# Pairwise products with batch statistics: the statistics computed with one shift per input, with half-sums on GpSimd

## The chip, the cores and the metric

The kernel runs on one core of one Trainium2 chip. The metric is device time in microseconds of one execution. A core has five engines that run side by side, each with its own instruction queue: TensorE (PE; its weight loads are shown as PEld), VectorE (DVE), ScalarE (ACT), GpSimd (POOL) and SyncE (SP), which here only issues transfers. Transfers run on 16 DMA engines. SBUF is the on-chip memory with 128 partitions; PSUM takes what TensorE makes.

## The reference

The inputs xi and xj are 1024 x 39 x 16 in float32. For each of the 741 pairs of a row r and a smaller column c, the outer product of xj[:, r] and xi[:, c] (16 x 16) is normalized over the batch and over both feature axes, scaled and shifted by gamma and beta of the pair, and multiplied by a 16 x 16 weight W:

```python
cross = xj[:, rows, :, None] * xi[:, cols, None, :]
mean = jnp.mean(cross, axis=(0, 2, 3), keepdims=True)
var = jnp.mean(jnp.square(cross - mean), axis=(0, 2, 3), keepdims=True)
normed = (cross - mean) * jax.lax.rsqrt(var + BN_EPS)
normed = normed * gamma[None, :, None, None] + beta[None, :, None, None]
out = normed[:, :, None, :, :] * W[None, None, :, :, :]
```

The output has 1024 x 741 x 256 values, 777 MB.

## The kernel before, in words

The batch lies as 128 partitions of NT = 8 rows each (index t), and is worked on T = 2 rows at a time. The kernel has two stages.

**Statistics.** The mean and variance of a product over the batch follow from small matrices of sums: per row t, the sum over the 16 features of each of the G = 38 used fields (`total`), and the sum of their squares. To keep the squares small, a shift per field is subtracted first; the shift is the field's mean over the rows t = 0. `sums` (L356) reduces the 16 features on VectorE. `deviation` (L366) subtracts the shift on GpSimd into a scratch tile; `square` (L375) squares that tile in place on ScalarE; `moments` (L381) sums the squares over the 16 features on VectorE; `means` (L388) makes the shifted means on VectorE. `gram` (L399) then accumulates three 38 x 77 matrices over the rows t on TensorE (`ps_g`). There are four pairs of rows for each of the two inputs, so eight deviations, squares and moments. From the three matrices a few 38 x 38 steps on ScalarE, GpSimd and VectorE (L478 to L508) make the mean and 1/std of every pair (`stq`), with one square root on ScalarE (L503).

**Spreading.** `spread` (L515) copies rows of that 38 x 38 table to all partitions with 76 matmuls in 12 groups, and `apply` (L531) combines a group with gamma and beta in `st_sb`. The first group (row 19) is needed first.

**Products.** A tile n holds T rows of the batch and the pairs of one row r: tile 0 to 3 are the row r = 19 (`mid`), later tiles other rows. `product` (L147) is one instruction of ScalarE or GpSimd: one row t and one feature i of xj times all r fields of xi. Tile 0 is special: its products are made from the raw xi while the statistics still run. These are 32 instructions of 128 x 304 elements, `raw0` on ScalarE (24 of them) and `raw0_pool` on GpSimd (8), handed out in portions by `emit` at places of the order that is written out by hand (L408 to L504). After `st_sb` is ready, `affine` (L241) scales and shifts tile 0 pair by pair on ScalarE, GpSimd and VectorE, and `weigh` (L254) multiplies by W on VectorE and stores in pieces. Since each raw product writes one feature of all 19 pairs, `affine` needs all 32. For later tiles `scale_xi` (L169) scales xi by the pair's factor on GpSimd, `products` (L183) multiplies on ScalarE and GpSimd, and `finish` (L276) adds the shift and multiplies by W, most of it on VectorE (L313), a share on GpSimd (L299, L302). `store` (L225) issues the output transfers on SP.

The order on every engine is that in which the program text issues instructions (`tc.manual_schedule()`); each engine works its queue in that order, so an instruction that waits holds up what stands behind it on its engine. Buffers are fixed: `y_sb` holds the output tiles in two halves, and the scratch of the statistics lies in the parts of it that the first tiles do not use yet. A transfer waits, before it is issued, for the transfer eight before it.

Input loads are issued on two queues: xj on SP, xi on ACT, between ScalarE's activations; gamma, beta and W also on ACT, after the fourth and fifth square (L449, L452).

Of the kernel before, what the change touches and what calls it, by code (L numbers as in the profile page):

```python
# [14 lines left out]
T = 2  # L15
# [12 lines left out]
LOADS = (1, 2, 3, 4, 6, 8)  # L28
# [15 lines left out]
def tile_pair_outer_batchnorm(  # L44
# [58 lines left out]
    place = {"dev": half * EE, "rest": (half + half // 2) * EE}  # L103
    stop = {"dev": (half + half // 2) * EE, "rest": 2 * half * EE}
# [18 lines left out]
    devs = [scratch("dev", P, T, G, E) for _ in range(7)]  # L123
# [5 lines left out]
    shift = scratch("rest", P, 2, G)  # L129
    shift_r = scratch("rest", G, 1)  # L130
    g1 = scratch("rest", G, 2 * G + 1)
    u_u, u_2 = (scratch("rest", G, 1) for _ in range(2))
    k, q1, q2, q3, uv, uv_2, v_half, mixed, low, mean, rstd, inv = (scratch("rest", G, G) for _ in range(12))
# [189 lines left out]
    with tc.manual_schedule():  # L323
        nc.gpsimd.memset(ones, 1.0)
        nc.sync.dma_start(xi_sb[:, 0, 0 : F // 2], xi_v[:, 0, 0 : F // 2])
        nc.scalar.dma_start(xi_sb[:, 0, F // 2 : F], xi_v[:, 0, F // 2 : F])
        nc.sync.dma_start(xj_sb[:, 0], xj_v[:, 0])
        def load(engine, to, source, t0, t1):
            engine.dma_start(to[:, t0:t1], source[:, t0:t1])

        for t0, t1 in zip(LOADS, LOADS[1:-2]):
            load(nc.sync, xj_sb, xj_v, t0, t1)
            load(nc.scalar, xi_sb, xi_v, t0, t1)


        nc.scalar.activation(shift_r, ones[0:G, 0:1], AF.Sqrt)
        load(nc.sync, xj_sb, xj_v, *LOADS[-3:-1])
# [12 lines left out]
        k_s = 1.0 / (P * E)  # L350
        sources = (xj_sb[:, :, 1:F], xi_sb[:, :, 0:G])

        def part(x):
            return slice(x * G, (x + 1) * G)

        def sums(t0, t1, xs=(1, 0)):  # L356
            for x in xs:
                nc.vector.tensor_reduce(  # L358
                    total[:, t0:t1, part(x)], sources[x][:, t0:t1], AX.X, ALU.add
                )  # L360

        steps = ((0, 1), (0, 0), (2, 1), (4, 1), (6, 1), (2, 0), (4, 0), (6, 0))

        def deviation(n):  # L366
            t0, x = steps[n]
            nc.gpsimd.tensor_tensor(  # L368
                devs[n % 7],
                sources[x][:, t0 : t0 + T],  # L370
                shift[:, x : x + 1, :].unsqueeze(3).to_broadcast([P, T, G, E]),
                ALU.subtract,
            )

        def square(n):  # L375

            _, x = steps[n]
            scale = 0.25 / NB**0.5 if x else 0.25
            nc.scalar.activation(devs[n % 7], devs[n % 7], AF.Square, scale=scale)  # L379

        def moments(n, t0, t1):  # L381
            first_t, x = steps[n]
            to = fb if x else fa
            nc.vector.tensor_reduce(  # L384
                to[:, t0:t1, G : 2 * G], devs[n % 7][:, t0 - first_t : t1 - first_t], AX.X, ALU.add
            )

        def means(t0, t1):  # L388
            for x, to in enumerate((fa, fb)):
                stt(  # L390
                    to[:, t0:t1, 0:G],
                    total[:, t0:t1, part(x)],
                    1.0 / (E * NB) if x else 1.0 / E,
                    ps_u[:, x : x + 1, :].to_broadcast([P, t1 - t0, G]),
                    ALU.mult,
                    ALU.subtract,
                )

        def gram(n, t0, t1):  # L399
            x = steps[n][1]  # L400
            for t in range(t0, t1):
                terms = ((0, fa[:, t, 0:G]), (2, ones[:, 0:G])) if x else ((1, fa[:, t, G : 2 * G]),)
                for acc, lhs in terms:
                    nc.tensor.matmul(  # L404
                        ps_g[acc][0:G, 0 : 2 * G + 1], lhs, fb[:, t], start=t == 0, stop=t == NT - 1
                    )

        raw0 = raw_products(0, nc.scalar, range(24))  # L408
        raw0_pool = raw_products(0, nc.gpsimd, range(24, 32))
        ps_shift = (ps_g[0][:, 0:G], ps_s[:, 0:G])  # L410
        for x in (1, 0):
            sums(0, 1, (x,))
            nc.tensor.matmul(ps_shift[x], ones, total[:, 0, part(x)], start=True, stop=True)
        nc.tensor.matmul(ps_c[0:G, 0:1], total[:, 0, 0:G], ones[:, 0:1], start=True, stop=True)

        ps_u = ps_s[:, 2 * G : 4 * G].rearrange("p (x f) -> p x f", x=2)
        nc.scalar.activation(shift[:, 1], ps_shift[1], AF.Copy, scale=k_s)
        nc.scalar.activation(ps_u[:, 1], shift[:, 1], AF.Copy, scale=1.0 / NB)
        load(nc.scalar, xi_sb, xi_v, *LOADS[-3:-1])
        load(nc.sync, xj_sb, xj_v, *LOADS[-2:])  # L420
        nc.scalar.activation(shift[:, 0], ps_shift[0], AF.Copy, scale=k_s)
        nc.scalar.copy(ps_u[:, 0], shift[:, 0])
        nc.scalar.activation(shift_r, ps_c[0:G, 0:1], AF.Copy, scale=k_s)

        def cell(n):
            return ps_c[0:G, 64 + n * G : 64 + (n + 1) * G]

        p_v_2, p_y, p_var, p_a, p_b = (cell(n) for n in range(5))
        u, v = shift_r, shift[0:G, 1, :]
        nc.scalar.activation(v_half, v, AF.Copy, scale=0.5)  # L430
        nc.scalar.activation(p_v_2, v, AF.Copy, scale=2.0)
        nc.scalar.activation(u_u, u, AF.Square)
        nc.scalar.activation(u_2, u, AF.Copy, scale=2.0)
        nc.scalar.activation(uv, v, AF.Copy, scale=u)
        nc.scalar.activation(uv_2, v, AF.Copy, scale=u_2)
        load(nc.scalar, xi_sb, xi_v, *LOADS[-2:])
        sums(1, 2)
        means(0, 2)
        sums(2, 3)
        sums(3, 4)  # L440
        means(2, 4)
        for n in range(7):
            deviation(n)
        emit(raw0, 2)
        for n in range(len(steps)):
            square(n)
            if n == 3:

                nc.scalar.dma_start(st_sb[:, 0], gamma.partition_broadcast(P))  # L449
                nc.scalar.dma_start(st_sb[:, 1], beta.partition_broadcast(P))  # L450
            elif n == 4:
                nc.scalar.dma_start(  # L452
                    w_sb[:, 0, :], w.rearrange("o i j -> (o i j)").partition_broadcast(P)
                )
            elif n < len(steps) - 1:
                emit(raw0, 2)

            t0 = steps[n][0]
            ends = (t0, t0 + 1, t0 + T) if n == len(steps) - 1 else (t0, t0 + T)
            for t0, t1 in zip(ends, ends[1:]):  # L460
                moments(n, t0, t1)
                gram(n, t0, t1)
            if n == 0:
                deviation(7)
            elif n == 1:
                sums(4, 6)
            elif n == 2:
                sums(6, 8)
                means(4, 8)
        emit(raw0_pool, 4)  # L470
# [6 lines left out]
        e_ab, e_a = g1[:, 0:G], g1[:, 2 * G : 2 * G + 1]  # L477
        nc.scalar.copy(g1, ps_g[0][0:G, 0 : 2 * G + 1])  # L478
        nc.scalar.activation(k, ps_g[2][0:G, 0:G], AF.Copy, scale=u)
        nc.scalar.activation(q1, v, AF.Copy, scale=e_a)  # L480
        nc.scalar.activation(q2, ps_g[2][0:G, G : 2 * G], AF.Copy, scale=u_u)
        nc.scalar.activation(q3, ps_g[0][0:G, G : 2 * G], AF.Copy, scale=u_2)
        emit(raw0, 3)
        nc.scalar.copy(w_dve, w_sb)
        emit(raw0, 4)
        nc.gpsimd.tensor_tensor(k, k, q1, ALU.add)
        nc.gpsimd.tensor_tensor(k, k, e_ab, ALU.add)
        nc.gpsimd.tensor_tensor(q2, q2, q3, ALU.add)
        nc.gpsimd.tensor_tensor(q3, uv_2, e_ab, ALU.mult)
        nc.gpsimd.tensor_tensor(q2, q2, q3, ALU.add)  # L490
        nc.gpsimd.tensor_tensor(q1, k, k, ALU.mult)
        nc.gpsimd.tensor_tensor(q2, q2, q1, ALU.subtract)
        nc.gpsimd.tensor_tensor(mean, k, uv, ALU.add)
        emit(raw0_pool, 4)

        stt(mixed, v_half, ps_g[1][0:G, 2 * G : 2 * G + 1], ps_g[1][0:G, 0:G], ALU.mult, ALU.add)
        nc.vector.tensor_mul(p_y, mixed, p_v_2)
        stt(low, ps_g[1][0:G, G : 2 * G], BN_EPS, q2, ALU.add, ALU.add)
        nc.vector.tensor_add(low, p_y, low)
        nc.vector.tensor_scalar_max(p_var, low, BN_EPS)  # L500

        nc.vector.reciprocal(inv, p_var)
        nc.scalar.activation(rstd, inv, AF.Sqrt)  # L503
        emit(raw0, 32)  # L504
        nc.vector.tensor_mul(p_a, p_var, rstd)
        stt(p_b, p_a, -0.5, rstd, ALU.mult, ALU.mult)
        stt(stq[:, 0], p_b, 1.5, rstd, ALU.add, ALU.mult)
        stt(stq[:, 1], mean, -1.0, stq[:, 0], ALU.mult, ALU.mult)  # L508

# [83 lines left out]
```

## Time and profile before

| | us |
|---|---|
| median of 4 runs | 1874.27 (1874.18 to 1874.43) |
| the profiled execution's own time | 1874.33 |
| its span, first to last instruction | 1872.6 |
| VectorE / ScalarE / GpSimd busy | 1723.0 / 1584.4 / 1550.9 |
| TensorE busy | 26.0 |
| read / written | 6.00 MB / 776.99 MB, 418 GB/s over the span |

The page gives busy time by engine, the span in 40 slices, the transfers, and groups of instructions by source line with mean duration and the idle time before them. The timeline lists instructions in order of time, neighbours of one line merged. "L153" is line 153 of the kernel; a line in a helper such as `product` stands for all its callers, which the operands tell apart: `y_sb<-xi_sb,xj_sb` on L153 is a raw product of tile 0, `y_sb<-xs,xj_sb` one of a later tile. `y_sb` as a destination of the first 30 us is mostly scratch.

### The profile page before, as it was taken

What the parts mean: (1) busy time and instruction counts of PE and PEld (TensorE: products, weight loads), DVE (VectorE), ACT (ScalarE), POOL (GpSimd) and SP (SyncE); (2) the same over time, 40 slices, a digit from 0 to 9 for tenths busy, and PEclk for the clock granted to TensorE, in tenths of its full rate; (3) what the DMA queues carried; (4) which work ended last, traced back from release to release, by engine and by line L of the source; (5) the groups of instructions that cost most, each with busy time, mean ns of one, the idle gap of its engine ahead of it and who ended that gap; (6) DMA issues with size and microseconds to landing.
All of it is one profiled execution on the core that took longest, in us unless ns stands there. A gap on an engine that the chain in (4) does not pass through costs nothing. (4 is left out here: it accounts for less than half of the span.)

```text
span 1872.6 us, 9236 instructions
## 1 busy us (share of the span) xinstructions
PE 26.0 (1%) x130; PEld 23.2 (1%) x130; DVE 1723.0 (92%) x2641; ACT 1584.4 (85%) x3152; POOL 1550.9 (83%) x1650
## 2 busy tenths in 40 slices
PE   5000000000000000000000000000000000000000
PEld 4000000000000000000000000000000000000000
DVE  8999888899999999999999999999999999999994
ACT  8999888898888877666798999999899998989892
POOL 9999877787777788999988888888888888888882
DMA  5999999999999999999999999999999999999998
GB/s 214 390 418 425 428 427 426 422 426 427 426 427 426 428 425 428 426 428 423 422 426 425 426 432 427 425 432 425 426 431 425 430 426 429 427 429 426 429 427 355
DMA packets 54711, 783.61 MB, mean 418 GB/s; under 512 B 4720, under 2 KB 6384, under 8 KB 17520
## 3 DMA queue, kind: packets, MB, share of 16 engines
q1 hardware_dynamic: 53344, 779.72, 98.2%
q10 hardware_dynamic: 1296, 3.29, 0.5%
q14 instruction: 70, 0.57, 0.1%
q8 instruction: 1, 0.02, 0.0%
HBM read 6.00 MB, written 776.99 MB: 418 GB/s over the span
## 5 line engine op out<-in xcount | busy, mean ns | idle before, releaser
L313 DVE SCALAR_TENSOR_TENSOR y_sb<-y_sb,st_sb,w_dve 128x512 f32<-128x512 f32 (+1 forms) x2511 | 1653.0, 738 | 114.4 <-issue 96.4
L153 ACT ACTIVATE y_sb<-xs,xj_sb 128x144 f32<-128x144 f32 (+23 forms) x2930 | 1453.3, 586 | 239.2 <-DMA out_dram<-y_sb 206.0
L302 POOL TENSOR_TENSOR y_sb<-y_sb,w_sb 128x2048 f32<-128x2048 f32 (+3 forms) x155 | 517.5, 3345 | 89.9 <-ACT y_sb L297 80.4
L155 POOL TENSOR_SCALAR y_sb<-xs,xj_sb 128x320 f32<-128x320 f32 (+19 forms) x1006 | 557.6, 578 | 9.1 <-DMA out_dram<-y_sb 9.0
L175 POOL TENSOR_TENSOR xs<-xi_sb,st_sb 128x640 f32<-128x640 f32 (+33 forms) x135 | 183.9, 1363 | 180.2 <-ACT y_sb L153 175.5
L299 POOL TENSOR_SCALAR y_sb<-y_sb,st_sb 128x512 f32<-128x512 f32 x291 | 196.8, 691 | 5.1 <-ACT y_sb L153 5.1
L297 ACT ACTIVATE y_sb<-y_sb,st_sb 128x512 f32<-128x512 f32 x160 | 100.2, 709 | 3.8 <-POOL y_sb L155 2.2
L208 POOL TENSOR_TENSOR y_sb<-xs,xj_sb 128x1280 f32<-128x1280 f32 (+2 forms) x24 | 66.6, 2798 | 0.0
L198 DVE TENSOR_TENSOR y_sb<-xs,ps 128x256 f32<-128x256 f32 (+3 forms) x32 | 24.8, 817 | 0.5
L522 PE MATMUL ps<-y_sb 38*128 38x38 f32 (+37 forms) x76 | 16.4, 397 | 3.1 <-DVE y_sb L508 3.1
L522 PEld LDWEIGHTS ps<-y_sb 38*128 38x128 f32 x76 | 16.3, 329 | 3.3 <-DVE y_sb L508 3.3
L379 ACT ACTIVATE y_sb<-y_sb 128x1216 f32<-128x1216 f32 x8 | 9.7, 1211 | 3.1 <-POOL y_sb L368 1.8
L153 ACT ACTIVATE y_sb<-xi_sb,xj_sb 128x304 f32<-128x304 f32 x24 | 11.4, 540 | 0.0
L384 DVE TENSOR_REDUCE y_sb<-y_sb 128x76 f32<-128x1216 f32 (+1 forms) x9 | 10.9, 1268 | 0.0
L259 DVE TENSOR_TENSOR y_sb<-y_sb,w_dve 128x2048 f32<-128x2048 f32 (+4 forms) x6 | 10.7, 1837 | 0.1
L368 POOL TENSOR_TENSOR y_sb<-xi_sb,y_sb 128x1216 f32<-128x1216 f32 x4 | 9.0, 2262 | 1.3 <-DMA xi_sb<-in_r_xi_dram 1.1
L358 DVE TENSOR_REDUCE y_sb<-xi_sb 128x38 f32<-128x608 f32 (+1 forms) x6 | 5.9, 990 | 3.9 <-DMA xi_sb<-in_r_xi_dram 3.9
L368 POOL TENSOR_TENSOR y_sb<-xj_sb,y_sb 128x1216 f32<-128x1216 f32 x4 | 9.0, 2265 | 0.0
L404 PE MATMUL ps<-y_sb 128*38 128x77 f32 x48 | 8.1, 337 | 13.4 <-DVE y_sb L384 13.2
L252 POOL TENSOR_SCALAR y_sb<-y_sb,st_sb 128x512 f32<-128x512 f32 x8 | 6.4, 812 | 2.0 <-ACT y_sb L153 2.0
L250 ACT ACTIVATE y_sb<-y_sb,st_sb 128x512 f32<-128x512 f32 x9 | 6.5, 799 | 0.2 <-ACT y_sb L153 0.2
L358 DVE TENSOR_REDUCE y_sb<-xj_sb 128x38 f32<-128x608 f32 (+1 forms) x6 | 5.9, 991 | 0.6 <-DMA xj_sb<-in_r_xj_dram 0.4
(60 smaller groups left out, 42.8 us busy)
## 6 DMA issues: line engine op xcount, KB each, us to landing
out_dram<-y_sb SPq DMA_DIRECT2D x16, 3072.0 KB, 21.7
out_dram<-y_sb SPq DMA_DIRECT2D x20, 2432.0 KB, 12.5
out_dram<-y_sb SPq DMA_DIRECT2D x10, 4608.0 KB, 15.1
out_dram<-y_sb SPq DMA_DIRECT2D x12, 3840.0 KB, 21.0
out_dram<-y_sb SPq DMA_DIRECT2D x16, 2816.0 KB, 22.3
out_dram<-y_sb SPq DMA_DIRECT2D x12, 3584.0 KB, 23.1
out_dram<-y_sb SPq DMA_DIRECT2D x12, 3328.0 KB, 24.3
out_dram<-y_sb SPq DMA_DIRECT2D x15, 2560.0 KB, 11.9
```

The costliest lines, as they stand in the source:

```text
L153: nc.scalar.activation(y, src, AF.Copy, scale=scale)
L155: engine.tensor_scalar(y, src, scale, 1.0, ALU.mult, ALU.mult)
L175: nc.gpsimd.tensor_tensor(xs, xi_sb[:, t0 : t0 + T, 0:r, :], s_sb[:, :, n0 : n0 + r, :].to_broadcast([P, T, r, E]), ALU.mult,)
L198: nc.vector.tensor_tensor(view(n)[:, t].rearrange("p n (i j) -> p n i j", j=E), xs[:, t].unsqueeze(2).to_broadcast([P, r, E, E]), xj_short ...
L208: nc.gpsimd.tensor_tensor(view(n)[:, t].rearrange("p n (i j) -> p n i j", j=E), xs[:, t].unsqueeze(2).to_broadcast([P, r, E, E]), xj_sb[:, ...
L297: nc.scalar.activation(y[:, :, c, :], y[:, :, c, :], AF.Identity, bias=t_c)
L299: nc.gpsimd.tensor_scalar(y[:, :, c, :], y[:, :, c, :], t_c, 1.0, ALU.add, ALU.mult)
L302: nc.gpsimd.tensor_tensor(y[:, :, c0:c1, :], y[:, :, c0:c1, :], w_sb.unsqueeze(1).to_broadcast([P, T, c1 - c0, EE]), ALU.mult,)
L313: stt(y[:, t : t + size, c, :], y[:, t : t + size, c, :], t_sb[:, n0 + c : n0 + c + 1], w_dve.to_broadcast([P, size, EE]), ALU.add, ALU.mult,)
L358: nc.vector.tensor_reduce(total[:, t0:t1, part(x)], sources[x][:, t0:t1], AX.X, ALU.add)
L368: nc.gpsimd.tensor_tensor(devs[n % 7], sources[x][:, t0 : t0 + T], shift[:, x : x + 1, :].unsqueeze(3).to_broadcast([P, T, G, E]), ALU.sub ...
L522: nc.tensor.matmul(ps[:, :, first[r] - n0 : first[r] - n0 + r], pick[:, r - 1, :], stq[:, :, 0:r], start=True, stop=True,)
```

## The change

**Shift.** One shift per input instead of one per field: the sum of t = 0 over the 38 fields is reduced once more (`first_total`), and a matmul with a matrix of ones and one column gives the total over the partitions. `offset` puts the negative shift into `bias_q`, and ScalarE's square reads xi or xj and takes it as its bias. The deviations are gone. `means` becomes an Identity activation on ScalarE with `bias_m`, once per pair of rows and input.

**Halves.** `fold` adds the upper 8 of 16 features to the lower 8 on GpSimd. It is applied to the raw inputs of the second and third pair of rows (`fold_sums`, four instructions) and to four of the eight square tiles (`fold_squares`); VectorE then sums 8 features instead of 16. The other sums and square sums stay as they were in size.

**Loads.** On ACT only xi of the rows t = 0 (second half), 1, 2 and 3. Everything else on SP: xj of 0 to 3, then xi of 4 and 5, xj of 4 and 5, xi of 6 and 7, xj of 6, xj of 7, gamma, beta, W.

**Table steps.** The 38 x 38 steps use scalars per row instead of some matrices; on VectorE there are three steps before the reciprocal instead of five.

**Raw products of tile 0.** ScalarE has 17 (24 before), GpSimd 15 (8 before). On ScalarE none is handed out between the squares; two come after the table steps, one before the square root, and 14 after it. On GpSimd 4 come before its table steps and 11 after.

From tile 0's affine on the program is the same. The core of the diff:

```diff
-LOADS = (1, 2, 3, 4, 6, 8)
+XI_BY_SCALAR = ((1, 2), (2, 3), (3, 4))
...
+        for t0, t1 in XI_BY_SCALAR:
             load(nc.scalar, xi_sb, xi_v, t0, t1)
+        for t in range(4):
+            load(nc.sync, xj_sb, xj_v, t, t + 1)
+        load(nc.sync, xi_sb, xi_v, 4, 6)
+        load(nc.sync, xj_sb, xj_v, 4, 6)
+        load(nc.sync, xi_sb, xi_v, 6, 8)
+        load(nc.sync, xj_sb, xj_v, 6, 7)
+        load(nc.sync, xj_sb, xj_v, 7, 8)
+        nc.sync.dma_start(st_sb[:, 0], gamma.partition_broadcast(P))
+        nc.sync.dma_start(st_sb[:, 1], beta.partition_broadcast(P))
+        nc.sync.dma_start(w_sb[:, 0, :], w.rearrange("o i j -> (o i j)").partition_broadcast(P))
...
+        def fold(to, of):
+            nc.gpsimd.tensor_tensor(to, of[..., 0:H], of[..., H:E], ALU.add)
+        def fold_sums(n, x):
+            half_of[n, x] = halves.pop()
+            fold(half_of[n, x], sources[x][:, pair(n)])
+        def means(n, x):
+            nc.scalar.activation(
+                moments[x][:, pair(n), 0:G], total[:, pair(n), part(x)],
+                AF.Identity, bias=bias_m[:, x : x + 1], scale=scale_m[x],
+            )
+        def square(n, x, t=slice(0, T)):
+            nc.scalar.activation(
+                squares[2 * n + x][:, t], sources[x][:, pair(n)][:, t],
+                AF.Square, bias=bias_q[:, x : x + 1], scale=scale_q[x],
+            )
+        def fold_squares(n, x):
+            sq = squares[2 * n + x]
+            fold(sq[..., 0:H], sq)
+        def seconds(n, x, t=slice(0, T), to=E):
+            nc.vector.tensor_reduce(
+                moments[x][:, pair(n), G : 2 * G][:, t], squares[2 * n + x][:, t, :, 0:to], AX.X, ALU.add,
+            )
...
-        raw0 = raw_products(0, nc.scalar, range(24))
-        raw0_pool = raw_products(0, nc.gpsimd, range(24, 32))
+        raw0 = raw_products(0, nc.scalar, range(17))
+        raw0_pool = raw_products(0, nc.gpsimd, range(17, 32))
         for x in (1, 0):
+            sums(slice(0, 1), x)
+            nc.vector.tensor_reduce(first_total[:, x : x + 1], total[:, 0, part(x)], AX.X, ALU.add)
+            nc.tensor.matmul(ps_shift[x], ones, first_total[:, x : x + 1], start=True, stop=True)
+        sums(slice(1, 2), 1)
+        sums(slice(1, 2), 0)
+        fold_sums(1, 1)
+        fold_sums(1, 0)
+        offset(1)
+        square(0, 1)
+        offset(0)
+        square(0, 0)
...
+        means(0, 1)
+        means(0, 0)
+        square(1, 1)
+        seconds(0, 1)
...
+        folded_sums(1, 1)
+        folded_sums(1, 0)
...
+        square(1, 0)
+        means(1, 1)
+        means(1, 0)
...
+        fold_squares(0, 0)
+        seconds(0, 0, to=H)
+        square(2, 1)
+        fold_squares(1, 1)
+        seconds(1, 1, to=H)
...
+        fold_sums(2, 1)
+        fold_squares(1, 0)
+        folded_sums(2, 1)
+        fold_sums(2, 0)
+        seconds(1, 0, to=H)
...
+        square(2, 0)
+        folded_sums(2, 0)
+        fold_squares(2, 1)
+        means(2, 1)
+        means(2, 0)
+        square(3, 1)
+        sums(pair(3), 1)
+        seconds(2, 1, to=H)
...
+        square(3, 0, slice(0, 1))
+        square(3, 0, slice(1, 2))
+        seconds(3, 1)
+        sums(pair(3), 0)
+        means(3, 1)
+        means(3, 0)
...
+        seconds(2, 0)
+        gram(1, (4, 5))
+        for t in range(T):
+            seconds(3, 0, slice(t, t + 1))
+            gram(1, (6 + t,))
         emit(raw0_pool, 4)
+        nc.scalar.copy(w_dve, w_sb)
+        nc.scalar.activation(v_ea, ps_g[0][0:G, 2 * G : 2 * G + 1], AF.Copy, scale=v)
...
+        nc.scalar.activation(q4, ps_g[0][0:G, 0:G], AF.Copy, scale=uv_2)
...
+        nc.gpsimd.tensor_scalar(mean, k, uv, 1.0, ALU.add, ALU.mult)
+        emit(raw0_pool, 32)
+        emit(raw0, 2)
...
+        nc.scalar.activation(vv_ea2, ps_g[1][0:G, 2 * G : 2 * G + 1], AF.Copy, scale=v_v)
+        stt(low, ps_g[1][0:G, G : 2 * G], BN_EPS, q1, ALU.add, ALU.add)
+        stt(low, ps_g[1][0:G, 0:G], v_2, low, ALU.mult, ALU.add)
+        nc.vector.tensor_scalar(p_var, low, vv_ea2, BN_EPS, ALU.add, ALU.max)
         nc.vector.reciprocal(inv, p_var)
+        emit(raw0, 1)
         nc.scalar.activation(rstd, inv, AF.Sqrt)
         emit(raw0, 32)
```

## The prediction

> **What bounds the kernel now.** I read the forty slices first, then busy time in a few stretches, and then the order of time in the first 60 us, engine by engine, because all lines of the change lie there. Times below are in us from the start of the span.
>
> The page of before, busy tenths in forty slices of 46.8 us each:
>
> ```profile
> DMA  5999999999999999999999999999999999999998
> GB/s 214 390 418 425 428 427 426 422 426 427 426 427 426 428 425 428 426 428 423 422 426 425 426 432 427 425 432 425 426 431 425 430 426 429 427 429 426 429 427 355
> ```
>
> The stores fill the DMA engines from the third slice to the last but one. Only the first two slices are below that. The next answer (us, then busy time and count on PE, PEld, DVE, ACT and POOL, the TensorE clock, DMA share, GB/s) splits them:
>
> ```profile
> 32.00:60.00 28.00, 15.80 (x75) 15.66 (x74) 27.59 (x51) 27.83 (x59) 26.47 (x38) 1.00 0.84 333
> 60.00:70.00 10.00, 0.00 (x0) 0.00 (x0) 9.97 (x18) 10.00 (x24) 9.12 (x13) 1.00 0.76 308
> 70.00:160.00 90.00, 0.00 (x0) 0.00 (x0) 88.69 (x143) 90.00 (x199) 88.67 (x107) 1.00 1.01 421
> ```
>
> From 32 to 70 ScalarE and VectorE are busy all the time and the DMA engines are not; from 70 on the transfers are the limit. So there is no slack behind tile 0: whatever moves the start of tile 0's affine work moves the end by as much. What sets that start is in the timeline (start, length, engine, line, operation):
>
> ```profile
> 21.02 6.77 DVE L384 TENSOR_REDUCE y_sb<-y_sb 128x76 f32<-128x1216 f32 x6
> 28.37 0.25 DVE L496 SCALAR_TENSOR_TENSOR y_sb<-y_sb,ps 38x38 f32<-38x38 f32 x1 [0.57 <-PE ps L404]
> 30.11 0.23 ACT L503 ACTIVATE y_sb<-y_sb 38x38 f32<-38x38 f32 x1
> 30.24 2.30 ACT L153 ACTIVATE y_sb<-xi_sb,xj_sb 128x304 f32<-128x304 f32 x5
> 32.38 0.17 DVE L540 TENSOR_TENSOR st_sb<-ps,st_sb 128x19 f32<-128x19 f32 x1
> 32.71 6.46 ACT L250 ACTIVATE y_sb<-y_sb,st_sb 128x512 f32<-128x512 f32 x9 [0.17 <-ACT y_sb L153]
> 32.80 4.16 POOL L252 TENSOR_SCALAR y_sb<-y_sb,st_sb 128x512 f32<-128x512 f32 x5 [1.96 <-ACT y_sb L153]
> 34.12 24.89 SPq L236 DMA_DIRECT2D out_dram<-y_sb  x14
> ```
>
> VectorE's sums run without a break to 27.8, the square root (L503) ends at 30.34, and the first group's scale and shift are ready at 32.55. At nearly the same moment, 32.54, ScalarE ends the last of tile 0's raw products (L153 from xi_sb). Two things must be there before the affine starts, and in before they arrive together. The bracket names the raw products as the later one.
>
> **The change, part by part.** *Subtraction dropped.* Eight GpSimd subtractions (L368, 2.26 each, 17.9) go; the shift becomes one number per input and sits in the bias of ScalarE's squares. VectorE's six means (L390, 1.3 in all) move to ScalarE as eight small activations. The first loads are issued as before, so the first sum again starts at 3.93. With one sum over 38 values more (not in the trace; between the 0.17 of L540 and the 0.39 of the reciprocal, I take 0.2), the one-column matmul and the offset, the first square starts near 5.8. It is not on the path.
>
> *Folds.* GpSimd now adds the halves of 16 values: eight instructions of 128x608 outputs, each with two full operands. No row has this form. The rows nearest to it are, of the groups of instructions (busy, mean ns of one, idle before):
>
> ```profile
> L302 POOL TENSOR_TENSOR y_sb<-y_sb,w_sb 128x2048 f32<-128x2048 f32 x68 | 307.1, 4531 | 82.7 <-ACT y_sb L297 80.4
> L302 POOL TENSOR_TENSOR y_sb<-y_sb,w_sb 128x512 f32<-128x512 f32 x28 | 35.6, 1270 | 2.3
> ```
>
> and, from the timeline:
>
> ```profile
> 36.93 1.22 POOL L175 TENSOR_TENSOR xs<-xi_sb,st_sb 128x608 f32<-128x608 f32 x1
> 13.58 4.48 POOL L368 TENSOR_TENSOR y_sb<-xi_sb,y_sb 128x1216 f32<-128x1216 f32 x2 [1.08 <-DMA xi_sb<-in_r_xi_dram]
> ```
>
> L175 has the right size (1.22), but one operand of L175 and L368 is a single value repeated over 16 elements. In L302 both operands change at every element, as in a fold, and it is dearer: (4531-1270)/1536 = 2.12 ns an element and 185 ns fixed, so 608 elements cost 1.47. Two in a row overlap by 0.04 (4.48 for two of 2.26), so one every 1.43. The far ends: 0.78 for a one-operand L155 of 608, and 2.26 for L368, if 1216 elements read counted as 1216. I take 1.43.
>
> The rule that speaks against this part is in the Trainium skill, GPSIMD Engine Reference, section 3.1: about 2.6 cycles an element for a two-input add, because both inputs share one read port, against about one on VectorE; elementwise work stays on VectorE. At its 1.2 GHz that is an estimate of 1.32 a fold without a fixed part; with seven folds 0.15 cheaper the sum below would end at 1876.1. L302 (2.12 ns) agrees with the rule and L175 (2.0 with its fixed part) does not show it; the row decides.
>
> When do they start? The first fold needs the third ACT-queue load (issued 2.20, 6.7 to landing: 8.9), so 9.0. I followed the five queues in the new order, and no fold then waits: the squares and loads that each needs are there 1 or more ahead. The seventh ends at 9.00 + 6 x 1.43 + 1.47 = 19.05, the eighth at 20.48.
>
> *VectorE's sums.* Up to there VectorE waits for folds. From 19.1 it has eight left and waits no more: of 608 elements one every 0.69 (8.68, 9.37, 10.06 in before; the 8-wide rows of a folded sum are not shown, bounds 0.69 and the 1.33 of 1216, and I take the row of the same element count), of 1216 one every 1.33. Three of the first and four of the second, 2.07 + 5.32, and the last takes 0.78: they end at 27.25, where before ended at 27.80. GpSimd's 1.43 buys VectorE 0.64 a fold. The tightest need is the third pair's xi square: ScalarE's in-order queue first waits for the means of the seventh fold's sums (20.0), then squares to 21.2, wanted at 21.8. Behind that wait stand the later squares and means; 0.5 of cover, after which each 0.1 costs 0.1.
>
> *The tail.* The last matmul ends 0.48 after its start, at 27.78 (28.33 in before). Two VectorE steps fewer, with q terms and vv_ea2 made beside: reciprocal done at 28.92, square root at 29.18 (30.34: there it stood behind a raw product). The remaining 2.2 to scale and shift are unchanged: ready at 31.35, which is 1.2 earlier.
>
> *Raw products.* ScalarE has 17 in place of 24, but none during the statistics: two after q4, one after vv_ea2, and 14 behind the square root, where before had 5. At one every 0.44 (2.30 for five) the first starts at 29.07, the last at 34.78, and it ends at 35.33. Every raw product writes all 19 pairs, so L250 on ScalarE, L252 on GpSimd and VectorE all queue behind it. GpSimd's 15 (4, then 11 at 0.49 from 27.85) end at 33.3. The statistics gain 1.2 and then wait 4.0 for ScalarE: the start moves from 32.54 to 35.33, +2.8.
>
> *Costed at nothing.* The loads: five transfers (late xi, gamma, beta, W) leave the ACT queue for SP, 13 issues of some 0.45 that wait only for loads landed by 9.4, all done long before the first store. The 6.0 MB read (in before up to 14.4 without a break at some 420 GB/s) land by about 18; xi of the last pair is wanted at 19.8, xj at 23, W at 24.7. If it came later, ScalarE's squares would be late one for one. ScalarE's some 25 small activations (0.2 each, one every 0.11) stand in its idle time at 17 to 20 and 22.6 to 24.6; its squares with a bias (1.21 without; with one, at most the 0.1 between L297 and L250 more) too. PE does 24 matmuls as before.
>
> Sum against the profiled execution: 1874.33 (span 1872.6 and 1.7 around it) + 2.8 = 1877.1. Its time is 0.06 above the median of the runs.
>
> **Rivals.** A: folds at the L175 price, one every 1.18. The path has seven of them ahead of VectorE's last stretch: -1.75, 1875.3 (+1.0). For it: same size, same 16-wide source. Against: the repeated operand. B: slower folds or another late link; one every 1.57 is 1878.0, 1.6 gives 1878.3, the far end 2.22 gives 1882.6. For it: 8-wide rows are new; against: L155 of 16-wide rows and L299 of 512-wide both take 0.69 for 512 elements, so row length costs nothing there. C, the other side: a fold at the one-operand price, one every 0.73; the sums then end 4.9 earlier, the raw products at 30.4, and the time is 1872.2. It decides from one fold every 1.03 down, where the 14 raw products end before 32.54. Against: no two-operand row is near it. D: the later start is made up before the transfers become the limit, and the time stays at 1874.3. For it: the DMA share of 0.76 at 60 to 70 is spare transfer time. Against: ScalarE has no idle time from 32 to 160, so its lateness stays.
>
> **How the numbers follow.** Forecast 0.60, A 0.17, B 0.15, C 0.04, D 0.04. A bound of 0.2%, 3.7 us, is about what a measurement tells from no change: 1870.5 to 1878.0. The forecast itself (1876.3 to 1878.0), A, C and D lie inside; B beyond it. Faster needs 3.7 us gained, more than C: 0.02. Slower: B and a tail of the forecast, 0.18. Same: 0.80. The range takes in A and the near part of B: 1874.9 to 1878.6.
>
> **What would show it.** Folds of 1.47 back to back from 9.0; VectorE's last moment sum ending near 27.3; square root at 29.2; st_sb's first group ready at 31.3 with VectorE idle 4 us behind it, ScalarE's raw products to 35.3; affine at 35.5; the first store at 36.9 in place of 34.12; the same row of stores after. I am wrong if folds wait for something, if the affine starts before ScalarE's last raw product, or if the stretch from 36 to 72 is shorter or longer than the one from 33 to 69.

## The result and the profile after

The changed kernel takes 1876.86 us (median of 41 runs, 1876.55 to 1877.98) against 1874.29 (61 runs, 1874.03 to 1874.96). The ratio is 1.0014, with a 95% interval of 1.0010 to 1.0018: 2.57 us slower, where 2.8 were forecast. The profiled execution took 1876.74 us, with a span of 1875.0 (before: 1874.33 and 1872.6), so the pair of profiles differs by 2.4.

The slices of the page of after (busy tenths of the DMA engines, then GB/s, 46.9 us each):

```profile
DMA  4999999999999999999999999999999999999998
GB/s 187 389 423 419 425 430 422 424 426 425 428 428 426 423 428 426 425 427 424 423 425 425 434 425 426 431 426 429 428 425 432 425 431 423 432 424 430 427 426 363
```

The first slice differs most: 187 GB/s where before had 214. The stretches of the prediction, three us later (us, then busy time and count on PE, PEld, DVE, ACT and POOL, the TensorE clock, DMA share, GB/s):

```profile
35.00:63.00 28.00, 14.91 (x70) 14.77 (x70) 27.11 (x48) 27.92 (x59) 26.50 (x38) 1.00 0.84 333
63.00:73.00 10.00, 0.00 (x0) 0.00 (x0) 9.97 (x18) 10.00 (x24) 9.09 (x13) 1.00 0.76 309
73.00:163.00 90.00, 0.00 (x0) 0.00 (x0) 88.69 (x143) 90.00 (x199) 88.67 (x107) 1.00 1.00 421
```

ScalarE's counts are those of before (59, 24, 199) and the DMA shares are 0.84, 0.76 and 1.00 against 0.84, 0.76 and 1.01. The program behind tile 0's affine runs as before, three us later. What decides lies ahead of it. From the timeline of after (start, length, engine, line, operation; in brackets the idle time before and what ended it):

```profile
8.93 1.46 POOL L375 TENSOR_TENSOR y_sb<-xi_sb 128x608 f32<-128x608 f32 x1 [3.34 <-DMA xi_sb<-in_r_xi_dram]
10.43 0.79 DVE L383 TENSOR_REDUCE y_sb<-y_sb 128x76 f32<-128x608 f32 x1 [1.49 <-POOL y_sb L375]
18.85 1.45 POOL L375 TENSOR_TENSOR y_sb<-y_sb 128x608 f32<-128x608 f32 x1
24.30 2.79 DVE L411 TENSOR_REDUCE y_sb<-y_sb 128x76 f32<-128x1216 f32 x3
27.95 5.45 POOL L157 TENSOR_SCALAR y_sb<-xi_sb,xj_sb 128x304 f32<-128x304 f32 x11
28.03 0.19 DVE L538 SCALAR_TENSOR_TENSOR y_sb<-ps,y_sb 38x38 f32<-38x38 f32 x1 [0.93 <-POOL y_sb L529]
29.24 0.23 ACT L544 ACTIVATE y_sb<-y_sb 38x38 f32<-38x38 f32 x1 [0.89 <-DVE y_sb L542]
29.38 6.24 ACT L155 ACTIVATE y_sb<-xi_sb,xj_sb 128x304 f32<-128x304 f32 x14
30.27 3.17 DVE L549 SCALAR_TENSOR_TENSOR y_sb<-y_sb 38x38 f32<-38x38 f32 x1
34.48 0.17 DVE L581 TENSOR_TENSOR st_sb<-ps,st_sb 128x19 f32<-128x19 f32 x1
35.70 6.46 ACT L252 ACTIVATE y_sb<-y_sb,st_sb 128x512 f32<-128x512 f32 x9
35.71 0.55 DVE L254 TENSOR_SCALAR y_sb<-y_sb,st_sb 128x512 f32<-128x512 f32 x1 [1.06 <-ACT y_sb L155]
37.14 21.76 SPq L238 DMA_DIRECT2D out_dram<-y_sb  x12
```

The sums end at 27.09 (27.80 before) and the square root at 29.47 (30.34). The affine nevertheless starts at 35.70 instead of 32.71, directly behind ScalarE's fourteen raw products (L155 from xi_sb, to 35.62). The first store follows at 37.14 instead of 34.12. One line was not in the forecast: L549, a step of 38 x 38 elements that took 0.19 before, takes 3.17 and makes st_sb ready at 34.65 instead of 31.35. VectorE's bracket on L254 says that it cost nothing here: VectorE still waited 1.06 us for ScalarE.

### The profile page after: what moved, and what is told of

Its sections match the earlier page's. It is cut to its first block, busy times and chain, and to the rows that moved or that the text cites. A ratio compares the mean times of both kernels' runs of the same rounds, so it can differ in the third digit from the quotient of the medians.

```text
span 1875.0 us, 9242 instructions
## 1 busy us (share of the span) xinstructions
PE 25.8 (1%) x128; PEld 22.9 (1%) x128; DVE 1720.1 (92%) x2633; ACT 1584.0 (84%) x3157; POOL 1547.5 (83%) x1655
## 4 chain that ended last, share of the span: by engine, by line
DMA 52%; ACT 18%; DVE 16%; issue 2%; POOL 1%; SPq 0%; ACTq 0%; DVEq 0%; POOLq 0%
DMA out_dram<-y_sb 52%; ACT y_sb L155 18%; DVE y_sb L315 16%; POOL y_sb L157 0%; POOL y_sb L304 0%; SPq L238 0%; ACT y_sb L299 0%; POOL xs L177 0%; DVE y_sb L200 0%; DVE xs L190 0%; ACTq L155 0%; DVEq L631 0%; DVE st_sb L581 0%; DVE ps L574 0%; DVEq L315 0%
## 5 line engine op out<-in xcount | busy, mean ns | idle before, releaser
L155 ACT ACTIVATE y_sb<-xs,xj_sb 128x144 f32<-128x144 f32 (+23 forms) x2930 | 1452.9, 586 | 238.9 <-DMA out_dram<-y_sb 191.7
L411 DVE TENSOR_REDUCE y_sb<-y_sb 128x76 f32<-128x608 f32 (+2 forms) x9 | 8.7, 990 | 1.9 <-POOL y_sb L375 1.9
L254 POOL TENSOR_SCALAR y_sb<-y_sb,st_sb 128x512 f32<-128x512 f32 x8 | 6.4, 814 | 2.4 <-ACT y_sb L155 2.4
L155 ACT ACTIVATE y_sb<-xi_sb,xj_sb 128x304 f32<-128x304 f32 x17 | 7.8, 535 | 0.0
L157 POOL TENSOR_SCALAR y_sb<-xi_sb,xj_sb 128x304 f32<-128x304 f32 x15 | 7.4, 513 | 0.0
L421 PEld LDWEIGHTS ps<-y_sb 128*38 128x38 f32 x48 | 5.6, 174 | 15.0 <-DVE y_sb L411 6.7
```

The costliest lines, as they stand in the source:

```text
L155: nc.scalar.activation(y, src, AF.Copy, scale=scale)
L157: engine.tensor_scalar(y, src, scale, 1.0, ALU.mult, ALU.mult)
L421: nc.tensor.matmul(ps_g[acc][0:G, 0 : 2 * G + 1], lhs, fb[:, t], start=t == 0, stop=t == NT - 1)
```

## The experiments

Two questions were open. Is it the raw products that set the end, and is the held step only beside them, or half the reason? And do the rewritten statistics gain anything? All eight kernels compute the full output, with every raw product and every sum. In the table, "affine" is the start of ScalarE's affine on tile 0 in the profile. The ratio is to before; for the eight kernels of the experiments it is to runs of before made beside them (median 1874.22 or 1874.23) and taken over all runs, so it is not exactly the quotient of the medians shown.

| kernel | median us | ratio, 95% interval | affine | median minus affine |
|---|---|---|---|---|
| before | 1874.29 | | 32.71 | 1841.6 |
| after | 1876.86 | 1.0014, 1.0010 to 1.0018 | 35.70 | 1841.2 |
| one operand in PSUM | 1876.85 | 1.0015, 1.0005 to 1.0024 | 35.90 | 1841.0 |
| ScalarE's raw products early | 1876.21 | 1.0010, 1.0001 to 1.0018 | 34.99 | 1841.2 |
| GpSimd's raw products early | 1876.77 | 1.0014, 1.0006 to 1.0023 | 35.64 | 1841.1 |
| both early | 1872.90 | 0.9995, 0.9986 to 1.0004 | 31.73 | 1841.2 |
| ScalarE early, one operand in PSUM | 1874.79 | 1.0002, 0.9993 to 1.0011 | 33.12 | 1841.7 |
| both early, no folds | 1872.42 | 0.9990, 0.9981 to 0.9999 | 31.14 | 1841.3 |
| before, with after's raw products | 1878.17 | 1.0021, 1.0013 to 1.0030 | 36.25 | 1841.9 |
| six folds, raw products early | 1870.49 | 0.9979, 0.9970 to 0.9988 | 29.17 | 1841.3 |

The last column is the main reading: over a spread of 7 us of the affine's start the rest of the program is the same within 1.0 us. What is gained or lost ahead of the affine arrives at the end. It is sharper still if each profiled execution's own time is taken in place of the median of all runs: 1841.0 to 1841.3 for after and the seven kernels built from it, 1841.6 for before and 1841.8 for the one built from before.

**One operand of the held step in PSUM.** A copy of the factor is made in PSUM, so that the held step (here L550) reads one operand from SBUF and one from PSUM:

```diff
-        p_var, p_a, p_b = (cell(n) for n in range(3))
+        p_var, p_a, p_b, p_s = (cell(n) for n in range(4))
...
+        stt(p_s, p_b, 1.5, rstd, ALU.add, ALU.mult)
         stt(stq[:, 0], p_b, 1.5, rstd, ALU.add, ALU.mult)
-        stt(stq[:, 1], mean, -1.0, stq[:, 0], ALU.mult, ALU.mult)
+        stt(stq[:, 1], mean, -1.0, p_s, ALU.mult, ALU.mult)
```

> The step that makes stq[:, 1] took 3.17 us in the changed kernel (0.19 before) and ended when GpSimd's eleven raw products ended. Theory: a VectorE instruction with both operands in SBUF is held while GpSimd works; here one operand comes from PSUM, so the step takes 0.2 us and the first group of st_sb is ready near 31.6 us in place of 34.65. The start of tile 0's affine is set by ScalarE's last raw product and stays at 35.7, so the time stays at 1876.9 within 0.4. Rival 1: the step waits for something else (the mean from GpSimd), and stays at 3.2. Rival 2: the hold is what sets the start; then the time falls by 0.5 or more.

From this kernel's timeline (columns as above):

```profile
28.14 5.44 POOL L157 TENSOR_SCALAR y_sb<-xi_sb,xj_sb 128x304 f32<-128x304 f32 x11
30.51 0.18 DVE L550 SCALAR_TENSOR_TENSOR y_sb<-y_sb,ps 38x38 f32<-38x38 f32 x1
31.74 0.17 DVE L582 TENSOR_TENSOR st_sb<-ps,st_sb 128x19 f32<-128x19 f32 x1
35.91 0.55 DVE L254 TENSOR_SCALAR y_sb<-y_sb,st_sb 128x512 f32<-128x512 f32 x1 [4.00 <-ACT y_sb L155]
```

GpSimd's raw products run as in after (5.44 against 5.45), the step takes 0.18, and st_sb is ready at 31.91, half a us after the 31.35 of the prediction. VectorE then waits 4.00 us for ScalarE, as the prediction said, and the time does not move. So the held step depends on where its operands lie, and in after it is hidden.

**ScalarE's raw products early.** They are handed out in the stretches in which after's ScalarE waits:

```diff
         means(1, 1)
+        emit(raw0, 1)
...
+        emit(raw0, 1)
         means(2, 1)
+        emit(raw0, 5)
...
         means(3, 1)
+        emit(raw0, 3)
...
         nc.scalar.copy(w_dve, w_sb)
+        emit(raw0, 1)
...
-        emit(raw0, 1)
+        emit(raw0, 2)
         nc.scalar.activation(rstd, inv, AF.Sqrt)
```

> ScalarE's 17 raw products are handed out in its idle stretches during the statistics (1, 1, 5, 3 and 1 ahead of activations that wait, 2 ahead of the square root), two stay behind the square root. Theory (the raw products behind the square root set the start): the last of them ends near 30.5, the start falls to the scale and shift, still held by GpSimd to about 34.7: affine near 34.8, 0.9 earlier, time 1875.9. Rival 1 (the late statistics set the start): no change, 1876.9. Rival 2 (the hold of the stq step is no hold and shrinks with it): affine at 33.5, when GpSimd's raw products end, 1874.7.

From the timeline of the kernel with ScalarE's raw products early:

```profile
28.13 5.45 POOL L157 TENSOR_SCALAR y_sb<-xi_sb,xj_sb 128x304 f32<-128x304 f32 x11
29.58 0.97 ACT L155 ACTIVATE y_sb<-xi_sb,xj_sb 128x304 f32<-128x304 f32 x2
30.46 3.15 DVE L554 SCALAR_TENSOR_TENSOR y_sb<-y_sb 38x38 f32<-38x38 f32 x1
34.66 0.17 DVE L586 TENSOR_TENSOR st_sb<-ps,st_sb 128x19 f32<-128x19 f32 x1
34.99 2.23 ACT L252 ACTIVATE y_sb<-y_sb,st_sb 128x512 f32<-128x512 f32 x3 [4.45 <-issue]
```

ScalarE's raw products now end at 30.55, five us earlier than in after, but the affine comes only 0.7 earlier. The held step (30.46 to 33.61, when GpSimd's eleventh product ends at 33.58) is now what the affine waits for. This is the wait that stood right behind the one I had forecast.

**GpSimd's raw products early.** Twelve of GpSimd's fifteen go ahead of its table steps, into the time in which it waits 4.07 us for ScalarE:

```diff
-        emit(raw0_pool, 4)
+        emit(raw0_pool, 12)
         nc.scalar.copy(w_dve, w_sb)
```

> GpSimd does 12 of its 15 raw products ahead of its table steps in place of 4. Theory: they fit in its idle 4 us there, so nothing is late; only 3 stand behind the table steps and end near 29.5, so the stq step (from 30.3) is not held and takes 0.2; st_sb's first group is ready near 31.5. ScalarE's raw products still end at 35.6, so the time stays at 1876.9 within 0.4. Rival: GpSimd's raw products or the hold set the start; then the time falls by 1 to 4.

From the timeline of the kernel with GpSimd's raw products early:

```profile
20.21 5.95 POOL L157 TENSOR_SCALAR y_sb<-xi_sb,xj_sb 128x304 f32<-128x304 f32 x12
27.89 1.50 POOL L157 TENSOR_SCALAR y_sb<-xi_sb,xj_sb 128x304 f32<-128x304 f32 x3
30.20 0.19 DVE L549 SCALAR_TENSOR_TENSOR y_sb<-y_sb 38x38 f32<-38x38 f32 x1
35.65 0.55 DVE L254 TENSOR_SCALAR y_sb<-y_sb,st_sb 128x512 f32<-128x512 f32 x1 [4.04 <-ACT y_sb L155]
```

With GpSimd idle from 29.39 on, the same step with both operands in SBUF takes 0.19. ScalarE's fourteen products still set the affine's start, and the time stays.

**Both early.** The two edits together:

> Both edits together. Theory: neither raw products nor the hold are left, the affine starts when the first group of st_sb is ready, near 31.6, which is 4.1 earlier than in the changed kernel and 1.1 earlier than before; time 1872.8, some 1.5 below before. Rival 1 (what is gained at the start is given back before the transfers become the limit): less than 2 gained, above 1875. Rival 2 (the raw products among the statistics delay the squares and sums): the last moment sum ends after 27.6 and the gain falls by as much.

From the timeline of the kernel with both early:

```profile
24.19 2.80 DVE L411 TENSOR_REDUCE y_sb<-y_sb 128x76 f32<-128x1216 f32 x3
30.16 0.19 DVE L554 SCALAR_TENSOR_TENSOR y_sb<-y_sb 38x38 f32<-38x38 f32 x1
31.40 0.17 DVE L586 TENSOR_TENSOR st_sb<-ps,st_sb 128x19 f32<-128x19 f32 x1
31.73 6.46 ACT L252 ACTIVATE y_sb<-y_sb,st_sb 128x512 f32<-128x512 f32 x9 [1.48 <-issue]
```

st_sb is ready at 31.57 and the affine starts at 31.73, 3.97 earlier than in after. The time falls by 3.96. Neither edit alone gave more than 0.7, since each left the other's wait in place.

**ScalarE early, one operand in PSUM.** The second edit with the first: the step is not held, and GpSimd's products stay late.

> ScalarE's raw products early, GpSimd's eleven late, and the stq step with one operand from PSUM. Theory: with the hold gone the scale and shift are ready near 31.8 us, and GpSimd's last raw product (33.5) is the latest of the three things the affine needs: affine near 33.8, 1.2 earlier than with ScalarE's early alone, time 1875.0. Rival (it was GpSimd's raw products and not the hold that set the start there): affine at 35.0, 1876.2.

From the timeline of this kernel, with ScalarE early and one operand in PSUM:

```profile
27.64 5.44 POOL L157 TENSOR_SCALAR y_sb<-xi_sb,xj_sb 128x304 f32<-128x304 f32 x11
30.01 0.18 DVE L555 SCALAR_TENSOR_TENSOR y_sb<-y_sb,ps 38x38 f32<-38x38 f32 x1
33.12 3.64 ACT L252 ACTIVATE y_sb<-y_sb,st_sb 128x512 f32<-128x512 f32 x5 [3.06 <-POOL y_sb L157]
```

The scale and shift are ready at 31.41 here. Now the affine waits for GpSimd's own last product, 33.08, because it needs all 32. In the profiled execution the input loads landed some 0.3 earlier than in after (its first fold starts at 8.61), and the affine followed the last product by 0.04 where 0.3 was expected: that is most of the 0.7 between the expected start of 33.8 and the 33.12 of the profile. The median, 1874.79, is 0.2 below what was expected. So ScalarE's products, the held step and GpSimd's products are three waits, one behind the other: in after they end at 35.62, 34.65 and 33.40.

**No folds.** The kernel with both early, and VectorE sums all 16 values everywhere:

```diff
-        fold_sums(1, 1)
-        fold_sums(1, 0)
...
-        folded_sums(1, 1)
+        sums(pair(1), 1)
...
-        fold_squares(0, 0)
-        seconds(0, 0, to=H)
+        seconds(0, 0)
```

and so on for the other folds.

> The kernel with both kinds of raw products early, without any of the eight folds: VectorE sums all 16 features. Theory (GpSimd's 1.42 us a fold is the limit up to 19 us, and VectorE's 0.64 saved a fold is less): VectorE is then busy from 7.5 without a break, its last moment sum ends near 26.2 in place of 26.9, the affine starts 0.7 earlier, near 31.0, time 1872.2. Rival (the folds pay): eight sums of 0.64 more, up to 5 us later, 1878.

From the timeline of the kernel without folds:

```profile
23.60 2.79 DVE L411 TENSOR_REDUCE y_sb<-y_sb 128x76 f32<-128x1216 f32 x3
31.14 6.46 ACT L252 ACTIVATE y_sb<-y_sb,st_sb 128x512 f32<-128x512 f32 x9 [1.48 <-issue]
```

VectorE's sums end at 26.39 without any help, against 26.99 with the eight folds, and the time is 0.5 lower (1872.42 against 1872.90, a difference near the noise; the affine's start, 31.14 against 31.73, agrees). The reason stands in after's timeline. VectorE waits 1.49 for the first fold and 0.62 to 0.64 for each of the next six, 5.3 in all. A folded sum behind such a wait takes its whole 0.79 in place of the 1.33 of a full sum in a row, so seven save 0.54 each, and the eighth, which need not wait, 0.64: 4.4. The difference, 0.9, is what the two timelines show: 19.56 from the first square sum (7.53) to the last sum's end in after, 18.71 (from 7.68) without folds.

**Before, with after's raw products.** Before's statistics are left as they are; the raw products get after's split (17 and 15) and after's late places:

```diff
-        raw0 = raw_products(0, nc.scalar, range(24))
-        raw0_pool = raw_products(0, nc.gpsimd, range(24, 32))
+        raw0 = raw_products(0, nc.scalar, range(17))
+        raw0_pool = raw_products(0, nc.gpsimd, range(17, 32))
...
-        emit(raw0, 2)
         for n in range(len(steps)):
...
-            elif n < len(steps) - 1:
-                emit(raw0, 2)
...
-        emit(raw0, 3)
         nc.scalar.copy(w_dve, w_sb)
-        emit(raw0, 4)
+        emit(raw0, 2)
...
-        emit(raw0_pool, 4)
+        emit(raw0_pool, 32)
...
+        emit(raw0, 1)
         nc.scalar.activation(rstd, inv, AF.Sqrt)
```

> The kernel before with nothing changed but the raw products of tile 0, which are shared out and placed as in the changed kernel: 17 on ScalarE, 2 after the table steps, 1 ahead of the square root and 14 behind it, 4 and 11 on GpSimd. Theory (the placing sets the start, whatever the statistics are): 14 raw products from 30.0 end at 36.2, affine near 36.4 in place of 32.7, 3.7 later, time 1877.9. The step at L508, with both operands in SBUF, is held until GpSimd's raw products end near 34.3, hidden behind ScalarE's. Rival (ScalarE, with fewer raw products among its squares, ends the statistics earlier): last moment sum before 26.8, time 1877 or less.

From the timeline of this variant of before:

```profile
28.76 5.44 POOL L155 TENSOR_SCALAR y_sb<-xi_sb,xj_sb 128x304 f32<-128x304 f32 x11
29.94 6.23 ACT L153 ACTIVATE y_sb<-xi_sb,xj_sb 128x304 f32<-128x304 f32 x14
30.82 3.43 DVE L505 SCALAR_TENSOR_TENSOR y_sb<-y_sb 38x38 f32<-38x38 f32 x1
36.25 1.52 ACT L250 ACTIVATE y_sb<-y_sb,st_sb 128x512 f32<-128x512 f32 x2
```

The loss appears without any of the new statistics: 3.9 us, and so does the held step. The sums end at 27.74, as in before (27.80), so the raw products among the squares had not delayed them. This kernel, after, "both early" and before make a square, though "both early" has after's split (17 and 15) and places of its own, not those of before. By the medians, late raw products cost 3.9 with the old statistics (1874.29 to 1878.17) and 4.0 with the new (1872.90 to 1876.86), and the new program gains 1.3 with late raw products (1878.17 to 1876.86) and 1.4 with early ones (1874.29 to 1872.90). After is the sum of the two: +3.9 and -1.3 give +2.6.

Not all of that gain is the statistics'. The affine's start moves by 3.5 (32.71 to 36.25) and 4.0 (31.73 to 35.70) for late raw products, but only by 0.6 (36.25 to 35.70) and 1.0 (32.71 to 31.73) for the new statistics. The other 0.4 to 0.8 of the gain lies behind the affine; it is taken up below, under the sum, and its cause is open. The interval of "both early" against before, 0.9986 to 1.0004, does not exclude no change in the time; the earlier affine is what shows the gain there.

**Six folds, raw products early.** The first two folds go (VectorE waited longest, 1.49, for the first); GpSimd takes 18 raw products, five of them before its first fold, and ScalarE 14, nearly all in its idle time:

```diff
-        raw0 = raw_products(0, nc.scalar, range(17))
-        raw0_pool = raw_products(0, nc.gpsimd, range(17, 32))
+        raw0 = raw_products(0, nc.scalar, range(14))
+        raw0_pool = raw_products(0, nc.gpsimd, range(14, 32))
...
-        fold_sums(1, 1)
-        fold_sums(1, 0)
+        emit(raw0_pool, 5)
+        emit(raw0, 1)
...
-        folded_sums(1, 1)
-        folded_sums(1, 0)
+        sums(pair(1), 1)
+        sums(pair(1), 0)
...
-        emit(raw0_pool, 4)
+        emit(raw0_pool, 12)
```

with `emit(raw0, n)` of 1, 1, 2 and 3 between the means, and 2 before the square root.

> Six folds in place of eight (the first pair of raw sums, which the whole chain of folds waited for, goes to VectorE unfolded), raw products 14 on ScalarE and 18 on GpSimd, all but two ahead of the square root. Theory: the first fold starts at 8.6 after five raw products, the chain is two folds shorter, and VectorE's last moment sum ends near 24.7; scale and shift ready near 29.0, affine near 29.2, 3.5 earlier than before, time 1870.3. Rival (ScalarE becomes the limit with its squares, means and raw products among each other): last moment sum after 25.5, 1871 or more.

From the timeline of the kernel with six folds:

```profile
8.61 1.46 POOL L375 TENSOR_TENSOR y_sb<-y_sb 128x608 f32<-128x608 f32 x1 [0.18 <-ACT y_sb L451]
14.84 0.79 DVE L411 TENSOR_REDUCE y_sb<-y_sb 128x76 f32<-128x608 f32 x1 [0.64 <-POOL y_sb L375]
21.63 2.79 DVE L411 TENSOR_REDUCE y_sb<-y_sb 128x76 f32<-128x1216 f32 x3
29.17 6.46 ACT L252 ACTIVATE y_sb<-y_sb,st_sb 128x512 f32<-128x512 f32 x9 [1.48 <-issue]
30.58 27.70 SPq L238 DMA_DIRECT2D out_dram<-y_sb  x15
```

VectorE waits for folds only three times (0.31, 0.64, 0.63) and its sums end at 24.42. Without folds they end at 26.39, with all eight at 26.99. The affine starts at 29.17 and the kernel takes 1870.49 us, 3.8 less than before and 6.4 less than after. Half-sums are worth having where VectorE has other sums to do while they are made.

## Why the prediction was right, and the step of it that was not

*The bound.* Right. The claim that there is no slack behind tile 0 is what the last column of the table shows, apart from about 0.5 late in the run (under the sum), and rival D (made up before the transfers are the limit) falls with it: the stores start 3.02 later, and the stretches of after hold the same work at the same DMA shares.

*The fold.* Right. The price taken from L302, 1.47 and one every 1.43, measured 1.46 and one every 1.42, back to back from 8.93 to 20.30. Rival A's price from L175 (1.22, where one operand is repeated) is refuted, so is C's, and B's slower folds too. The 8-wide rows cost VectorE what the element count says: 0.79, one every 0.69. The estimate from the Trainium skill (GPSIMD Engine Reference, section 3.1: 2.6 cycles an element) was 1.32 without a fixed part and is 0.14 below what was measured; its advice, elementwise work on VectorE, is borne out here against the eight folds (sums to 26.99 with them, 26.39 without) and not against six (24.42).

*The sums.* Right. The last eight start at 18.93 and end at 27.09, without a pause between them (forecast 19.1 and 27.25). The cover for the square wanted at 21.8 held: it ended at 21.30, and VectorE read it at 21.65 without a wait.

*The tail.* A third of a us off up to the square root. The prediction had the q terms made beside, at no cost. Here VectorE's first step waits until GpSimd ends the last of its table steps (L529, at 27.97), 0.35 after the last matmul (27.62). With that and steps of 0.25 instead of 0.2 the reciprocal ends at 29.21 instead of 28.92 and the root at 29.47 instead of 29.18.

**The step that failed** is "The remaining 2.2 to scale and shift are unchanged: ready at 31.35". They were ready at 34.65. I had carried 0.19 for L508 over from before, where GpSimd had ended its four raw products at 30.83, ahead of the step at 31.14. With eleven behind the table steps GpSimd was at work until 33.40, and the step had both operands in SBUF. Both facts were at hand: the prediction itself had GpSimd's products until 33.3, and in the timeline of before L508 reads y_sb alone. It had counted only the waits of one engine for another's result. The two lines of before:

```profile
28.84 1.99 POOL L155 TENSOR_SCALAR y_sb<-xi_sb,xj_sb 128x304 f32<-128x304 f32 x4
31.14 0.19 DVE L508 SCALAR_TENSOR_TENSOR y_sb<-y_sb 38x38 f32<-38x38 f32 x1
```

The error cost nothing in after, since the wait of 4.0 for ScalarE became 3.17 of hold and 1.06 of wait, with the same end. It leaves st_sb 3.3 late, and where ScalarE's products are early, as in the second experiment, that is the affine's start.

*The raw products.* Right. Fourteen at one every 0.44, from 29.38 to 35.62 (forecast 29.07 to 35.33), affine at 35.70 (35.5), first store at 37.14 (36.9).

*The sum.* The forecast had +2.8; the affine moved by 2.99 (the tail's 0.3 in it), the profiled time by 2.4, the median by 2.57. The affine came 0.2 later than the sum had it, and about 0.5 comes back late in the run, which the prediction did not have: that the time is within 0.3 of the forecast is in part luck. In the timeline of before and then of after, VectorE's longest pause near 1330 us:

```profile
1332.46 4.70 DVE L313 SCALAR_TENSOR_TENSOR y_sb<-y_sb,st_sb,w_dve 128x512 f32<-128x512 f32 x7 [1.94 <-issue]
```

```profile
1334.58 4.70 DVE L315 SCALAR_TENSOR_TENSOR y_sb<-y_sb,st_sb,w_dve 128x512 f32<-128x512 f32 x7 [1.01 <-issue]
```

The same seven instructions stand 2.12 apart there, not 3.0, because after pauses for 1.01 where before pauses for 1.94. The pause is 1.91 in the kernel built from before, and 0.99 to 1.01 in all seven built from after. So this gain goes with the changed program and not with the places of the raw products: in the profiled executions after and the seven kernels built from it take 0.4 to 0.6 less from the affine to the end than before, and the one built from before 0.2 more. What ends the pause the profile does not say ("issue"), and it was not settled.

## What to carry to other kernels

When a change moves independent filler work behind the critical chain, add up the filler on each engine to its end and compare that with the chain's end: here the chain gained 1.0 us (the affine at 31.73 in "both early", 32.71 in before) and the late filler cost 4.0 (35.70). Take the price of a new instruction from a row with the same kind of operands (both read in full), not from the row of the same size. And remove waits together: three of them stood one behind the other here, and no single edit showed more than 0.7 of the 4.0.

## What the runs showed of the hardware

A VectorE step whose two operands are both in SBUF was held for as long as GpSimd worked back to back on its raw products: 3.17, 3.15 and 3.43 us in three kernels, ending 0.03 to 0.05 after GpSimd's last one. That is not one GpSimd instruction (0.49) but the six or seven that were left. With one operand in PSUM, in the same company, it took 0.18 (two kernels), and with GpSimd idle 0.19 (before and four kernels). VectorE's sums, which read one tensor, were not held beside GpSimd's folds and products: 1.41 for 1216 elements throughout after.

The Trainium skill (SBUF — State Buffer, section "Who interferes with whom") says that a VectorE instruction with two inputs in SBUF contends with a GpSimd instruction that reads SBUF, that the ports the two share are an exclusive lock, and that the order of issue decides who blocks. The runs agree on who is held and on the way out through PSUM; that the loser waits for a whole series they add. GpSimd's instructions get longer too: beside the affine of after, VectorE's L254 started at 35.71 and took 0.55, and GpSimd's first L254, started at 35.79, took 1.03 where most of its eight took 0.76. VectorE's second L254, started at 36.90 behind a GpSimd L254 of 36.81, took 0.95. Both fit the order of issue, but what lengthened them, and why VectorE's step is not let in between two of GpSimd's raw products, was not tried.
